# Transposes of the output rows in the places of u and v, and a later start for one row's sums and the other row's scores

## The chip, the cores and the metric

The kernel runs on one core of a Trainium2 chip. The time is the device time of one execution in microseconds (us). Before the change the median of three runs is 1711.06 us (1710.57 to 1711.61). The engines are TensorE (PE, its weight loads PEld), VectorE (DVE), ScalarE (ACT), GpSimd (POOL) and SyncE (SP), which issues most of the transfers.

## The reference

Sixteen rows of 512 positions by 512 features go through two layers, each added to its input.

```python
# layer 0: two dense layers; the last 128 outputs come from the row's own expert
h = gelu(einsum('bnd,hd->bnh', x, fc1_w) + fc1_b)             # hidden 2048
shared = einsum('bnh,sh->bns', h, fc2_w) + fc2_b               # 384 outputs
expert = einsum('bnh,bph->bnp', h, experts_w[idx]) + experts_b[idx]  # 128 outputs
x = x + concatenate([shared, expert], -1)
# layer 1: attention pooling with one score per position
scores = einsum('bsa,a->bs', tanh(einsum('bsd,da->bsa', x, W1) + b1), v)
mask = where(pt == 0, l <= j, where(pt == 1, l >= j, l != j))  # per row one of three
p = softmax(where(mask, scores[:, None, :], -1e30), -1)
x = x + einsum('bjl,bld->bjd', p, x) / mask.sum(-1)
```

All of it is float32. The masked softmax has only prefix, suffix and all-but-one forms, so the pooling is written as recurrences along the positions (scans on VectorE) and no product of 512 by 512 is made.

## The kernel before

**Groups.** Rows are worked in pairs, eight groups of an *elder* row (`b0`) and a *younger* row (`b0 + 1`). The products use a seven-product scheme for 2 by 2 blocks (1, 5, 6, 2, 7, 3, 4 in the order of work), so operands need sums and differences, made on VectorE or GpSimd. A group has a first stage (lines 1456 to 1506: seven outer by seven inner products, Gelu into `hT`) and a second one. In groups 1 to 6, called joint, the second stage has an upper part for both rows at once (`Joint.upper`, steps u0 to u13) and then for each row five products named 5, 7, 6, 3 and 4 (`Joint.row`). "Row 0" and "row 1" below are these row parts of the elder and the younger row. Groups 0 and 7 use `fc2` instead.

**One product of a row** (line 1004) is 32 matmuls into one bank: 16 with the shared weights (m = 0) and 16 with the row's expert weights (m = 1). In the middle of each half and between them a callback runs, named by the product and a letter: `5a` after a quarter, `5m` after half, `5c` after three quarters, and `5` after the outputs have been taken. What the callback `at_row` issues stands at that place in every engine's queue. The whole order is written out by hand: each engine works strictly in the order in which the program issues, and only semaphores are inserted.

**What the callbacks issue.** `joined.outer(r, k)` (line 982) makes row r's four moving operands, one VectorE instruction of 128x2048 each (line 987): k = 0 for product 5, 1 for product 7, 2 for product 6, 3 for product 4. `sum1` (line 519) and `sums` (lines 522 to 530) make the expert's weight sums; `sums("a11", h)` is needed by the m = 1 halves of 7 and 6, `sums("a12", h)` by that of 3. Both take a tile from the ring. `residual` (line 714) loads a piece of the input on ScalarE's queue and adds the bias there. The row's four output quarters are written at lines 1012, 1027, 1031 and 1034 into `x1T`, of which there are two buffers.

**The ring.** Weight tiles of 256 KB come through ten buffers in the order of one written plan (`Ring`, lines 176 to 198); a freed buffer lets SP issue the next load of the plan. SP's queue also holds the stores of the outputs and, once per group, the eight loads of the next group's `x` (`Moving`, line 290), whose place comes free with line 1012 of row 1.

**Pooling.** A row's `Pooling` begins with `project` (line 1059, eight matmuls and a tanh on ScalarE) and `score` (line 1069, two matmuls, two copies into `srow`, a transfer into `s2`). The rest is a generator. Its first part makes coefficients with many small VectorE instructions, stores them (`co`, lines 1290 and 1291) and reads them back broadcast to all partitions (`cb`, line 1295; a copy at 1298). Then, for four chunks of the features, come `weigh` (1326 on VectorE, 1329 on ScalarE), `recur` (1337, a scan, then 1363 and 1364 on ScalarE) and `finish` (1345 and 1355), each step fed by the one before. Last come two small instructions on GpSimd (1388, 1389) and, for rows below 13, four transposes on VectorE (`flip`, line 1405), each with four stores of 64 KB in packets of 128 bytes (line 1410).

The generator is advanced by `slot(budget, passed)`: each yielded number is a cost against the budget, a negative number a pause. The tables `SPARE`, `JOINT_0` and `JOINT_1` give the budgets per place, and only the oldest pooling advances. `drain(left)` issues at once all that is left: `drain(1)` just before row 0 ends the previous group's elder pooling, and `drain()` just after row 0's last product ends the previous group's younger one. The elder row of the current group is projected and scored within row 1, the younger one in the first block of the next group's first stage.

**Where the transposed chunks are put.** `flip` takes a tile of tag `yo` of which there are two buffers. The two `srow` tiles of a pooling have the same tag, and one of them is kept until the maximum search of that pooling (lines 1194 and 1196). The tags `u` and `v` are tiles of 128 x 1024, one buffer each, used by `weigh` and `recur`.

Of the kernel before, what the change touches and what calls it, by code (L numbers as in the profile page):

```python
# [9 lines left out]
F32 = mybir.dt.float32  # L10
# [7 lines left out]
def tile_cond_experts_then_prompt_pool(  # L18
# [17 lines left out]
    P = 128  # L36
    B, _, ND, S = xT.shape
# [21 lines left out]
    p1 = ctx.enter_context(tc.tile_pool(name="p1", bufs=1))  # L59
# [12 lines left out]
    LOWER = ("s1", "s3", "s2", "s4", "a22")  # L72
# [5 lines left out]
    def joint(i):  # L78
        return 0 < i < B // 2 - 1
# [95 lines left out]
    class Ring:  # L175
        def __init__(self):
            self.plan, self.tiles = [], {}
            for i in range(B // 2):
                b = 2 * i
                for o in OUTER:  # L180
                    self.plan += [("f1", i, o, p) for p in (INNER if i else INNER_0)]
                if joint(i):
                    ex = lambda r, o: [("ex", b + r, o, h) for h in range(2)]
                    lo = lambda r, names: [("lo", b + r, n, h) for n in names for h in range(2)]
                    u = [("u2", b, o, n) for o in ("a11", "a12") for n in UPPER]
                    self.plan += u[:10] + ex(0, "a11") + u[10:]
                    for r in range(2):
                        self.plan += (ex(1, "a11") if r else []) + lo(r, LOWER[:1]) + ex(r, "a12") + lo(r, LOWER[1:])
                    continue
                for r in range(2):  # L190
                    self.plan += [("up", b + r, "a11", h) for h in range(4)]
                    if not r:
                        self.plan += [("ex", b, "a11", h) for h in range(2)]
                    self.plan += [("up", b + r, "a12", h) for h in range(4)]
                    self.plan += [("ex", b + r, "a12", h) for h in range(2)]
                    self.plan += [("lo", b + r, n, h) for n in LOWER for h in range(2)]
                    if not r:
                        self.plan += [("ex", b + 1, "a11", h) for h in range(2)]
            self.at = 0
            self.taken, self.free = [], set()  # L200
# [346 lines left out]
    ex = const.tile([SG, 96], F32, name="ex")  # L547
# [166 lines left out]
    def residual(b, r, c):  # L714
        t = p1.tile([P, 2, HC], F32, tag="xr", name=f"xr_{b}_{r}{c}", bufs=2)
        nc.scalar.dma_start(t, xT[b][:, ts(r, 2), ts(c, HC)])

        def ready():
            for m in range(2):
                oc = 2 * r + m  # L720
                bias = fc2b_sb[:, oc : oc + 1] if oc < NS else be[:, b : b + 1]
                nc.scalar.activation(t[:, m, :], t[:, m, :], AF.Identity, bias=bias)  # L722
            return t

        return ready
# [320 lines left out]
    class Pooling:  # L1046
# [101 lines left out]
        def run_all(self):  # L1148
            yield from self.weights()
            yield from self.apply()  # L1150
            if self.b < B - 3:
                yield -2
                for dc in range(ND):
                    store = self.flip(dc)
                    yield 0.7
                    yield -1
                    store()
                    yield -1

        def weights(self):  # L1160
            V, b = nc.vector, self.b
# [239 lines left out]

        def flip(self, dc, yo=None):
            if yo is None:
                yo = p1.tile([P, S], F32, tag="yo", name=f"yo_{self.b}_{dc}", bufs=2)
            nc.vector.transpose(yo, self.x1T[:, dc, :])  # L1405
            to = out[self.b].rearrange("(c j) (k a i) -> k a j c i", j=32, a=4, i=32)

            def store():
                for a in range(4):
                    nc.sync.dma_start(to[dc, a], yo[ts(a, 32), :].rearrange("j (c i) -> j c i", i=32))  # L1410

            return store
# [15 lines left out]
    def drain(left=0):  # L1428
        while sum(not p.done for p in pools) > left:
            slot(1e9, 1e9)  # L1430
# [7 lines left out]
    }  # L1438

    JOINT_0 = {"5c": 1.0, "5": 2.0, "7c": 1.5, "7": 2.5, "6a": 1.5, "6m": 2.5, "3a": 1.5, "3m": 1.0, "3": 2.0}  # L1440
    JOINT_1 = {"5": 1.5, "7a": 1.5, "7c": 1.2, "7": 1.5, "6a": 1.5, "6": 0.4, "4a": 1.2}

    LAST_2 = {n + q: 1.7 for n in "57633" for q in ("a", "m", "c", "")}
    LAST_2.update({"6": 0.4, "3a": 0.8, "3m": 0.8})
    pool = xi_after = None
    for i in range(B // 2):
# [4 lines left out]
        experts = Expert(b0)  # L1451
# [4 lines left out]
        for n in range(7):  # L1456
# [8 lines left out]
            for k in range(14):  # L1465
# [28 lines left out]
                if n == 6 and joint(i):  # L1494
                    if k == LAG:
                        joined = Joint(b0, hT)
# [18 lines left out]
        if joint(i):  # L1515
            nxt, xr = {}, {}

            def at_upper(name):
                if name == "u0":
                    joined.sum("a11", 2)  # L1520
                elif name == "u1":
                    for h in range(2):
                        experts.sum1(h)
                elif name == "u2":
                    xr_next[:] = [t() for t in xr_next]
                elif name == "u4":
                    joined.outer(0, 0)
                elif name == "u7":
                    xr["22"], xr["12"] = residual(b0, 1, 1), residual(b0, 0, 1)
                elif name == "u8":  # L1530
                    joined.outer(0, 1)
                elif name in ("u9", "u10"):
                    experts.sums("a11", int(name[1:]) - 9)
                elif name in ("u11", "u12"):
                    n = ("22", "12")[int(name[1:]) - 11]
                    xr[n] = xr[n]()
                    slot(1.2, 1.7)

            def at_row(r, name):
                if name == "5m":  # L1540
                    joined.outer(r, 2)
                elif name == "7m":
                    joined.outer(r, 3)
                if r == 0:
                    if name == "5a":
                        for h in range(2):
                            experts.sums("a12", h)
                    elif name == "7":
                        nxt["ex"] = Expert(b0 + 1)
                        for h in range(2):  # L1550
                            nxt["ex"].load(h)
                    elif name == "6c":
                        joined.outer(1, 0)
                    elif name == "3m":
                        for h in range(2):
                            nxt["ex"].sum1(h)
                    elif name == "3c":
                        joined.outer(1, 1)
                    elif name == "4m":
                        for h in range(2):  # L1560
                            nxt["ex"].sums("a11", h)
                    elif name == "4a":
                        for n in ("22", "12"):
                            nxt[n] = nxt[n]()
                    slot(JOINT_0.get(name, 0.0), 1.7)
                    return
                if name == "5a":
                    pool.project()
                    nxt["x"] = Moving(i + 1)
                elif name == "5m":  # L1570
                    pool.score()
                    pools.append(pool)
                    for h in range(2):
                        experts.sums("a12", h)
                elif name == "6m":
                    nxt["xi"] = nxt["x"].inner_sums(0, nc.vector)
                    nxt["x"].outer_sum(1, nc.vector)
                elif name == "3m":
                    nxt["xi_2"] = nxt["x"].inner_sums(1, nc.vector)
                slot(JOINT_1.get(name, 0.0), 1.7)  # L1580

            def after(r):
                if r == 0:
                    nxt["22"], nxt["12"] = residual(b0 + 1, 1, 1), residual(b0 + 1, 0, 1)
                else:
                    b = b0 + 2
                    xr_next[:] = [residual(b, 0, 0), residual(b + 1, 0, 0) if joint(i + 1) else residual(b, 1, 1)]

            ba = joined.upper(xr_next, at_upper)
            drain(1)  # L1590
            for r in range(2):
                x1T = joined.row(
                    r, ba[r], experts, nxt if r else xr, lambda name: at_row(r, name), lambda: after(r)
                )
                if r == 0:
                    experts = nxt["ex"]
                    drain()
                before_last, pool = pool, Pooling(b0 + r, x1T)
            x_next, xi_next, xi_after = nxt["x"], nxt["xi"], nxt["xi_2"]
            continue  # L1600
        for row in range(2):
            b = b0 + row
            more = row == 1 and b + 1 < B
            nxt = {}
# [68 lines left out]
            if row == 0:  # L1673
                experts = nxt["ex"]
# [3 lines left out]
            before_last, pool = pool, Pooling(b, x1T)  # L1678
# [46 lines left out]
```

## Time and profile before

| what | value |
|---|---|
| median of three runs | 1711.06 us |
| the profiled execution's own time, and its span | 1713.13 us, 1711.3 us |
| TensorE busy, its weight loads | 1580.4 us, 1313.3 us |
| VectorE busy | 1242.7 us |
| ScalarE busy, GpSimd busy | 626.5 us, 453.5 us |
| mean granted TensorE clock | 0.964 |
| VectorE's idle time ahead of line 1405, put down to the stores | 105.0 us in 33 waits |
| ScalarE's idle time ahead of line 1012, put down to line 1405 | 82.3 us in 5 waits |

A line of the groups or of the timeline reads: line, engine, operation, output<-inputs, shape, count, busy time, and in brackets the idle time of the engine ahead of it with what ended it. The waits list sums such idle time by who waited for whom. A wait for several things is put down to the one that came last. Names stand without their numbers: `w_lo_s` is any tile of the ring for the products 5, 7, 6 and 3 of a row, `pa` the projection's bank, `psc` the score's.

### The profile page before, as it was taken

Reading aid. Unit: us, or ns where it says so; the run is one execution under the profiler, and the core shown is the slowest. Engines: PE = TensorE matmul, PEld = TensorE weight load, DVE = VectorE, ACT = ScalarE, POOL = GpSimd, SP = SyncE. Lnnn points to the kernel's source line nnn. Section 1 sums busy time; section 2 is a strip of 40 time slices with the busy share of each in tenths; the row PEclk is TensorE's granted clock in tenths of the full one; section 3 lists DMA queues with packets and bytes.
Section 4 is the critical chain, followed back from the end, with each engine's and each line's share of the span. In section 5 each row is a group of like instructions: output and inputs, shape, how many; then the busy total and the mean of one; then the engine's idle time right before and its main releaser. Section 6 shows DMA issues by size and latency. Waiting matters only on the chain. (4 is left out here: it accounts for less than half of the span.)

```text
span 1711.3 us, 22082 instructions
## 1 busy us (share of the span) xinstructions
PE 1580.4 (92%) x6890; PEld 1313.3 (77%) x6890; DVE 1242.7 (73%) x2200; ACT 626.5 (37%) x1304; POOL 453.5 (26%) x440
## 2 busy tenths in 40 slices
PE   8999999999999699997999979999699987998996
PEld 6788888877888488875888758887588875886784
DVE  7885668766887659866598665986659877586686
ACT  2441246322561325513265022641226412363323
POOL 5631045000631016300263001620117201260020
PEclk9999999999999899998999989999899998999997
DMA  7768646546556375563655636556365664555442
GB/s 261 239 203 273 219 129 175 173 127 223 152 155 179 91 235 153 160 175 93 226 150 168 184 95 212 148 170 193 85 205 148 178 179 126 181 149 155 141 118 49
DMA packets 344768, 285.60 MB, mean 167 GB/s; under 512 B 145356, under 2 KB 262156, under 8 KB 344652
## 3 DMA queue, kind: packets, MB, share of 16 engines
q1 hardware_dynamic: 313388, 241.09, 48.9%
q10 hardware_dynamic: 24864, 21.04, 3.8%
q0 software_dynamic: 6400, 22.07, 3.6%
q8 instruction: 55, 0.90, 0.2%
q14 instruction: 61, 0.50, 0.1%
HBM read 252.50 MB, written 31.55 MB: 166 GB/s over the span
## 5 line engine op out<-in xcount | busy, mean ns | idle before, releaser
L633 ACT ACTIVATE hT<-hT,fc1b_sb 128x256 f32<-128x256 f32 x416 | 181.2, 501 | 59.8 <-DVE hT L687 34.5
L674 POOL TENSOR_TENSOR q<-p,hT 128x512 f32<-128x512 f32 x80 | 105.5, 1320 | 347.0 <-ACT p L667 346.6
L616 PE MATMUL bx<-xi,w_f_s_s 128*128 128x256 f32 x512 | 128.0, 382 | 3.3 <-DVE by L671 1.7
L1405 DVE STREAM_TRANSPOSE yo<-x1T 128x512 f32<-128x512 f32 x60 | 41.2, 701 | 107.4 <-DMA out_y<-yo 105.0
L616 PEld LDWEIGHTS bx<-xi,w_f_s_s 128*128 128x128 f32 x512 | 96.0, 190 | 21.5 <-issue 3.6
L671 DVE TENSOR_TENSOR by<-bx,p 128x512 f32<-128x512 f32 x112 | 77.4, 691 | 39.3 <-PE bx L616 38.7
L616 PE MATMUL bx<-xi,w_f_a_s 128*128 128x256 f32 x384 | 97.3, 386 | 3.2 <-POOL xi L337 2.6
L1337 DVE TENSOR_TENSOR_SCAN f<-cb,u 128x512 f32<-128x512 f32 x60 | 81.8, 1363 | 22.3 <-ACT u L1329 21.6
L1063 PE MATMUL pa<-x1T,w_sb 128*128 128x512 f32 x120 | 65.7, 687 | 33.9 <-DVE x1T L1034 32.1
L646 DVE TENSOR_TENSOR hT<-bx,hT 128x512 f32<-128x512 f32 x112 | 75.1, 682 | 23.1 <-PE bx L616 23.0
L1146 POOL TENSOR_TENSOR xm<-x1T,is 128x4 f32<-128x4 f32 x15 | 5.3, 352 | 310.2 <-DVE wt L1210 263.7
L1004 PE MATMUL bd<-hT,e 128*128 128x256 f32 x384 | 86.8, 379 | 0.0
L667 ACT COPY p<-bd 128x512 f32<-128x512 f32 x112 | 65.3, 583 | 58.5 <-PE bd L616 57.2
L616 PEld LDWEIGHTS bx<-xi,w_f_a_s 128*128 128x128 f32 x384 | 71.7, 191 | 19.1 <-POOL xi L337 4.8
L1345 DVE TENSOR_TENSOR f<-v,cb 128x512 f32 x60 | 54.1, 902 | 41.6 <-ACT v L1364 41.6
L1004 PEld LDWEIGHTS bd<-hT,e 128*128 128x128 f32 x384 | 73.0, 190 | 9.9
L646 DVE TENSOR_TENSOR hT<-by,hT 128x512 f32<-128x512 f32 x112 | 75.0, 681 | 3.7 <-PE by L616 1.3
L722 ACT ACTIVATE xr<-xr,fc2b_sb 128x256 f32<-128x256 f32 x96 | 44.3, 502 | 85.9 <-DMA xr<-in_xT 30.1
L1363 ACT ACTIVATE v<-f,U,cb 128x512 f32<-128x512 f32 x60 | 48.8, 813 | 69.6 <-DVE U L1338 68.8
L1063 PEld LDWEIGHTS pa<-x1T,w_sb 128*128 128x128 f32 x120 | 25.0, 215 | 61.7 <-DVE x1T L1034 37.0
L687 DVE TENSOR_TENSOR hT<-bx,q 128x512 f32<-128x512 f32 x80 | 54.6, 682 | 18.8 <-PE bx L616 17.2
L662 ACT COPY ba<-bx 128x512 f32<-128x512 f32 x32 | 18.3, 571 | 133.3 <-PE bx L616 110.5
(351 smaller groups left out, 3938.9 us busy)
## 6 DMA issues: line engine op xcount, KB each, us to landing
w_lo_s<-w2s_s SPq DMA_DIRECT2D x128, 256.0 KB
w_f_s_s<-w1s_s_s SPq DMA_DIRECT2D x112, 256.0 KB
w_f_a_s<-w1s_a_s SPq DMA_DIRECT2D x84, 256.0 KB
w_f_s_a<-w1s_s_a SPq DMA_DIRECT2D x84, 256.0 KB
w_f_a_a<-in_fc1T SPq DMA_DIRECT2D x69, 256.0 KB
w_ex_a<-in_fc2T SPq DMA_DIRECT2D x64, 256.0 KB
xr<-in_xT ACTq DMA_DIRECT2D x64, 256.0 KB
out_y<-yo SPq DMA_DIRECT2D x240, 64.0 KB
```

What stands on the lines that cost most here:

```text
L616: nc.tensor.matmul(to.rearrange("p (b s) -> p b s", b=2) if len(mv.shape) == 3 else to, w[:, ts(2 * mh + m, P)], mv, start=(not add and m ...
L633: nc.scalar.activation(to[:, m], src[:, m], AF.Gelu, bias=fc1b_sb[:, hc + m : hc + m + 1])
L646: eng.tensor_tensor(to, src, self.place(prev, r, c, mh)[1], ALU.add)
L667: nc.scalar.copy(u["p5"], bd)
L671: add(u["y"], u["x"], u["p5"], ALU.add)
L674: nc.gpsimd.tensor_tensor(self.both(u["q"]), self.both(u["p5"]), self.place(self.to[0][1], 1, 1, mh)[1], ALU.add)
L687: add(to, self.both(u["x"]), self.both(u["q"]), ALU.add)
L1004: nc.tensor.matmul(bank[:, m, :], ex.of(n)[:, k, :] if m else as_chunks(lo[k // 4])[:, k % 4, :], mv[:, k, :], start=(not add and m == 0 a ...
L1063: nc.tensor.matmul(pa, w1_sb[:, dc, :], self.x1T[:, dc, :], start=(dc == 0), stop=(dc == ND - 1))
L1337: V.tensor_tensor_scan(f[dc], c0, turned(u[dc]), 0.0, ALU.mult, ALU.add)
L1345: V.tensor_tensor(f[dc], turned(v[dc]), beta, ALU.mult)
L1363: nc.scalar.activation(v[dc][:, :S], f[dc], AF.Identity, bias=U[:, dc : dc + 1], scale=fac)
```

## The change

The transposes get a new place: chunks 0 and 1 share one tile of tag `u`, chunks 2 and 3 one of tag `v`, so `yo` is left to the score rows (and to the start and the last row). The pause after each store is gone. For a group's younger row, `outer(1, 1)`, which row 0's product 3 used to issue, is issued in row 1's product 5 (at 5a), and the expert's a11 sums move from row 0's product 4 to row 1's 5m; `outer(1, 2)` moves from 5m to 5c and the a12 sums from 5m to 7c. The plan of the ring puts the a11 tiles of the younger row behind its s1 tiles, and the a12 tiles behind s3. The elder row's projection moves from 5a to 5m and its score from 5m to 7a, and the budgets of row 1 follow.

```diff
@@ Ring.__init__
-                    for r in range(2):
-                        self.plan += (ex(1, "a11") if r else []) + lo(r, LOWER[:1]) + ex(r, "a12") + lo(r, LOWER[1:])
+                    self.plan += lo(0, LOWER[:1]) + ex(0, "a12") + lo(0, LOWER[1:])
+                    self.plan += lo(1, LOWER[:1]) + ex(1, "a11") + lo(1, LOWER[1:2]) + ex(1, "a12") + lo(1, LOWER[2:])
@@ Pooling.run_all
                     store()
-                    yield -1
@@ Pooling.flip
-                yo = p1.tile([P, S], F32, tag="yo", name=f"yo_{self.b}_{dc}", bufs=2)
+                if dc % 2 == 0:
+                    self.yo = p1.tile([P, 2, S], F32, tag=("u", "v")[dc // 2], name=f"yo_{self.b}_{dc}")
+                yo = self.yo[:, dc % 2, :]
@@ budgets
-    JOINT_1 = {"5": 1.5, "7a": 1.5, "7c": 1.2, "7": 1.5, "6a": 1.5, "6": 0.4, "4a": 1.2}
+    JOINT_1 = {"5": 1.5, "7": 1.5, "6a": 1.5, "6": 0.4, "3a": 1.2, "4a": 1.2}
@@ at_row
-                if name == "5m":
-                    joined.outer(r, 2)
-                elif name == "7m":
+                if name == "7m":
                     joined.outer(r, 3)
                 if r == 0:
-                    if name == "5a":
+                    if name == "5m":
+                        joined.outer(r, 2)
+                    elif name == "5a":
...
-                    elif name == "3c":
-                        joined.outer(1, 1)
-                    elif name == "4m":
-                        for h in range(2):
-                            nxt["ex"].sums("a11", h)
...
                 if name == "5a":
-                    pool.project()
+                    joined.outer(r, 1)
                     nxt["x"] = Moving(i + 1)
                 elif name == "5m":
+                    pool.project()
+                    for h in range(2):
+                        experts.sums("a11", h)
+                elif name == "5c":
+                    joined.outer(r, 2)
+                elif name == "7a":
                     pool.score()
                     pools.append(pool)
+                elif name == "7c":
                     for h in range(2):
                         experts.sums("a12", h)
```

## The prediction

> **What bounds the kernel now.** First the page's busy shares and the clock row.
>
> ```profile
> span 1711.3 us, 22082 instructions
> PE 1580.4 (92%) x6890; PEld 1313.3 (77%) x6890; DVE 1242.7 (73%) x2200; ACT 626.5 (37%) x1304; POOL 453.5 (26%) x440
> PEclk9999999999999899998999989999899998999997
> ```
>
> TensorE carries the kernel, and its granted clock dips at regular places. The last chain (section 4 of the page) covers only the tail, so I went to the waits of TensorE alone:
>
> ```profile
> PE psc L1072 <- ACT aT L1067: 36.8, 6, 7.5
> PE pa L1063 <- DVE x1T L1034: 32.1, 6, 6.5
> PE ba L1004 <- DVE hT L987: 15.8, 6, 3.6
> PE bc L766 <- DMA w_lo_s<-w2s_s: 8.1, 1, 8.1
> ```
>
> Columns: total us, times, longest. Three waits come once in each of the six joint groups, 84.7 us in all; the fourth is in group 7. Where they come from is seen in the timeline of one group (group 2: start, us, engine, idle before it and its releaser):
>
> ```profile
> 524.35 3.62 PE L1004 MATMUL bc<-t,w_lo_s 128*128 128x256 f32 x16
> 536.15 0.71 DVE L1405 STREAM_TRANSPOSE yo<-x1T 128x512 f32<-128x512 f32 x1 [3.64 <-DMA out_y<-yo]
> 540.30 3.72 PE L1004 MATMUL ba<-hT,w_lo_s 128*128 128x256 f32 x16 [1.97 <-DVE hT L987]
> 553.99 0.37 SPq L1295 DMA_DIRECT2D cb<-co_d  x1
> 561.15 1.05 ACT L1298 COPY cb<-cb 128x1024 f32<-128x1024 f32 x1 [12.13 <-DMA cb<-co_d]
> 562.83 0.67 DVE L1326 TENSOR_TENSOR u<-x1T,cb 128x512 f32<-128x512 f32 x1
> 565.94 0.61 ACT L1329 ACTIVATE u<-u 128x512 f32<-128x512 f32 x1
> 570.22 0.68 DVE L1034 TENSOR_TENSOR x1T<-bd,u 128x512 f32<-128x512 f32 x1
> 570.96 3.70 PE L1063 MATMUL pa<-x1T,w_sb 128*128 128x512 f32 x4 [6.23 <-DVE x1T L1034]
> 583.63 1.87 PE L1072 MATMUL psc<-aT,v_sb 128*1 128x512 f32 x2 [7.25 <-ACT aT L1067]
> 585.42 5.02 PE L1004 MATMUL bc<-t,es 128*128 128x256 f32 x16
> 590.28 3.62 PE L1004 MATMUL bd<-hT,w_lo_s 128*128 128x256 f32 x16
> 593.10 0.71 DVE L1405 STREAM_TRANSPOSE yo<-x1T 128x512 f32<-128x512 f32 x1 [3.29 <-DMA out_y<-yo]
> 618.20 1.03 PE L616 MATMUL bx<-xT,w_f_a_a 128*128 128x256 f32 x4
> ```
>
> Row 0's products start at 524.35. Meanwhile VectorE is held in the transposes of the previous group's elder row, each waiting for the store before it (4.22, 3.31 and 3.64 us), and is free only at 536.9. From there it runs without a gap to 562.8, so all of row 0's work is late: TensorE waits 1.97 us for a difference, the younger pooling's coefficients go out at 553.99, and L1034 comes at 570.22. The projection waits for it. The score then waits for a tanh that ScalarE has behind the drained pooling. The transposes after 584.84 wait for stores again.
>
> A product is two halves of 3.45 us; ten of them, a projection (3.60) and a score (1.02) are 73.6 us. Group 2 took 618.20 - 524.35 = 93.85. The same difference, from the same lines, is 80.2, 95.65, 95.9, 96.7 and 93.7 us for groups 1, 3, 4, 5, 6.
>
> **The change part by part.**
>
> *Transposes into u and v.* Each group's elder drain loses three waits on stores. Its four transposes (0.65 us apart) now end behind the last upper addition (L976, released by TensorE's end at 524.35): about 526.5 instead of 536.9. The younger drain loses 2.97 + 3.29. The new owners wait for nothing: the last readers of u and v are the steps just before on VectorE and ScalarE, and the next weighing comes tens of us after the stores.
>
> *The dropped pause* shortens the elder pooling in the budget tables, but followed slot by slot it only moves its first transpose from the last block of stage one to u11; the younger's steps in row 0 keep their slots in groups 2 to 6. In group 1 they come some eight slots earlier. Worth nothing by itself in 2 to 6; its cover is the 89 us of stage one.
>
> *Row 0, group 2, with VectorE 10.4 us earlier.* Same durations: expert sums 1.25, L987 2.27, steps 1.7, p5x 0.6, steps 2.0, L987 2.27, steps 1.2 end at 537.7; then L1019 waits for TensorE (product 7 ends 538.2), and the remaining 4 us of coefficients end at 543. TensorE no longer waits and ends product 6 at 545.1; SP then issues two loads and the broadcast at 546.3 (553.99 before). It took 7.2 us to its copy, so cb is ready at 554.6. Residuals: L1024 frees their place at 546 instead of 555.3, so they land 9.2 us earlier and ScalarE weighs at 556.7 (565.94). Sums and difference (2.4 + 2.27) are gone from ahead of it. So L1034 moves by 9.2 to 561.0.
>
> *Row 1.* It starts at 558.9. The projection stands after 16 matmuls (562.4), its second half at 564.2: L1034 is done, that wait is gone. The score stands in product 7, behind a tanh ready by 574: gone. **The stall goes to product 7.** Its operand, outer(1, 1), is now issued after the whole drain. L1034 to the drain's first transpose took 584.84 - 570.22 = 14.6 us; four transposes 2.65, L987 2.3: ready at 561.0 + 19.5 = 580.5. TensorE is there at 558.9 + 6.9 + 3.6 = 569.4, so it waits 11.1 us. Queued behind the moved difference on VectorE are the expert sums (2.5), outer(1, 2) (2.3), p5x, the a12 sums and outer(1, 3): all end within 9 us, and the second half of product 7, product 6 and product 3 need theirs 3.4, 8.9 and 16 us on.
>
> *Clock.* After the 7.25 us wait, the score took 1.87 for 1.02 and the next half product 5.02 for 3.62: 2.25 us lost. After 3.44 us in group 3, 5.41 for 3.62; after 3.64 in group 4, nothing. The Trainium skill (TensorE: Matmul & The Clock Gate, Part 1: The HAM clock gate) has half clock after an idle window of about 3.4 us and until a busy one: 1.7 us per long wait however long it is, by its free-running window more or less. Row and rule are near; I take 2.3 by the row (the rule gives 0.6 less per group). One long wait in place of two pays it once.
>
> So row stage = 45.0 + 11.1 + 2.3 + four products 27.6 + score 1.0 = **87.0 us**. For groups 2 to 6: 475.8 before - 435.0 = 40.8 saved. In group 1 the pooling is one chunk further, its drain ends about 369, outer(1, 1) at 371, and TensorE needs it at 373.9: all 6.4 us over 73.6 vanish.
>
> *Loads.* In the new plan s4 and a22 of the younger row stand on SP behind 16 stores and 8 loads of x. Stores: 16 took 9.49 us in group 1; from 576.3 to 586, x to 590, s4 by 591.5. TensorE needs s4's halves at 597 and 598.7. In group 1's trace a22, issued behind x at 394.26, had its second half awaited at 403.8, 9.5 us on: that would be 600, a wait of 1.4. The skill (DMA: Bandwidth & Descriptors, Queues, rings and completion order) has SP own one row of rings and the engines take turns between rows: only the 2.6 MB ahead on SP's own row count in full, at the 320 to 400 GB/s of group 1's windows 7 to 8 us after x's first issue and some start-up: 595 to 596, no wait. The expert gathers that shared group 1's engines come later here. I take half, 0.7 us for six groups: 4 lost. Bounds 0 and 4 us a group.
>
> x itself lands by 596 and is needed in VectorE's 6m step; hidden. ScalarE's copies of scores (11 us behind stores before) are free; nobody waits.
>
> *Elder steps later* (new budgets in row 1): some 10 small VectorE steps and the issues of co move to the first block of stage one; the broadcast comes 3 slots later and is needed 8 slots after that. Nothing; without that cover the 7 us of a broadcast.
>
> *Group 7.* TensorE's 8.1 us wait is for two loads behind 16 stores, which took 15.69 us gated by transposes; ungated about 10, so 5 of 8.1 come back. 5 us.
>
> Sum: 40.8 + 6.4 - 4 + 5 = 48. The profiled execution's own time is 1713.1 (1.8 around its span): 1665.1. It lies 2.1 above the median of the runs, so on their scale **1663 us**.
>
> **Rivals.**
> 1. *The younger chain comes forward by half only*, because broadcast and residuals, now in the traffic of denser stores, take longer than 7.2 and 8.4 us. For: those two, not VectorE, released the chain. Against: engines moved 60 to 70% then. Each us is one us in five groups: 4.6 x 5 = 23, so 1686.
> 2. *s4 comes late* by its upper bound, 4 us a group: 20 more, 1683. For: the order on SP; against: the bytes.
> 3. *Slower: the transposes still wait*, since two share one place; if the order is kept for a whole tile, the second waits for the first one's store. Elder drain: some 7 us kept, so the chain comes 7 later; younger drain: 6.3 kept in front of outer(1, 1). Row stage 87.0 + 13.3 = 100.3, 5.1 over the mean of 95.2: +26 in five groups; group 1 gains 3, group 7 some 2, loads cost 4: 1736. It decides from 8.2 us of kept waits a group. Against: at 562.85 half of the projection ran on two quarters of x1T with L1034 unwritten, so order is kept for parts of a tile.
> 4. *Better*: product 7 waits only 8 us, loads cost nothing: 1644.
> 5. *Nothing moves*: the stall at product 7 equals the two removed.
>
> **How the numbers follow.** Likeliest 54% (own range 1648 to 1678: 3 us a group either way), rival 1 15%, rival 2 11%, rival 3 or a stall of like size 13%, rival 4 4%, rival 5 3%. Leaving out rival 3, the far end of rival 1 and the best of rival 4 gives 1645 to 1698. A difference within 0.2%, 3.4 us, can't be told from none. Faster: 54 + 15 + 11 + 4 = 84%; same 3%; slower 13%.
>
> **What would show it.** L1405 without waits on out_y; no wait at L1063 and L1072; L1004's bd of row 1 waiting about 11 us for L987 in groups 2 to 6, none in group 1; L1034 some 37 us after row 0's start (46 now); row stages near 87. Wrong if L987 is awaited 18 us or more, if bc of row 1 waits for a DMA of w_lo, or if L1405 still waits.

## The result and the profile after

The changed kernel takes **1728.17 us** (median of four runs, 1727.85 to 1730.19) against 1710.82 beside it: a ratio of 1.0109 with a 95% interval of 1.0094 to 1.0124. It is slower by some 17 us where 1663 was forecast, so the prediction was wrong in sign.

The head of the page after, the same three rows as before:

```profile
span 1726.2 us, 22078 instructions
PE 1572.7 (91%) x6890; PEld 1313.5 (76%) x6890; DVE 1236.0 (72%) x2200; ACT 622.0 (36%) x1304; POOL 430.5 (25%) x440
PEclk9999999999999899998999989999899998999997
```

Nothing shows in the shares; the clock row has as many dips as before. TensorE's waits (total us, times, longest) show what changed places:

```profile
PE bd L1004 <- issue: 63.3, 5, 13.8
PE bc L1004 <- DMA w_lo_s<-w2s_s: 21.2, 5, 5.9
PE pa L1063 <- DVE x1T L1034: 15.4, 5, 3.5
PE bc L766 <- DVE ml L1184: 7.2, 1, 7.2
...
PE psc L1072 <- ACT aT L1067: 2.1, 1, 2.1
```

The tanh wait (36.8 before) is down to 2.1, and the wait for differences in row 0 is gone. The new first line is product 7 of row 1: no releaser is named, but its matmul starts 0.11 us after the moved difference ends (586.50 + 2.25 against 588.86, below). The second line is product 3 of row 1 waiting for an s4 tile (s4 are its shared weights, a22 those of product 4); that wait did not exist before. The third was to vanish and has halved.

Group 2 in the timeline of TensorE and SP (start, us, engine, line, operation; idle before and releaser in brackets). Row 0 starts at 527.33, and a time with a plus sign below is counted from the start of row 0:

```profile
527.33 3.62 PE L1004 MATMUL bc<-t,w_lo_s 128*128 128x256 f32 x16
...
552.39 0.94 SPq L238 DMA_DIRECT2D w_ex_a<-in_fc2T  x2
553.42 0.45 SPq L1289 DMA_DIRECT2D co_d<-co  x1
...
556.67 0.32 SPq L1294 DMA_DIRECT2D cb<-co_d  x1
...
569.49 0.68 DVE L1034 TENSOR_TENSOR x1T<-bd,u 128x512 f32<-128x512 f32 x1
570.22 1.98 PE L1063 MATMUL pa<-x1T,w_sb 128*128 128x512 f32 x4 [3.02 <-DVE x1T L1034]
...
584.83 13.89 SPq L1412 DMA_DIRECT2D out_y<-yo  x16
...
586.50 2.25 DVE L987 TENSOR_TENSOR hT<-hT 128x2048 f32<-128x2048 f32 x1
...
588.86 3.75 PE L1004 MATMUL bd<-hT,w_lo_s 128*128 128x256 f32 x8 [13.20 <-issue]
...
598.82 4.05 SPq L262 DMA_DIRECT2D xT<-in_xT  x8
...
602.97 0.90 SPq L236 DMA_DIRECT2D w_lo_s<-w2s_s  x2
...
610.48 6.59 PE L1004 MATMUL bc<-hT,w_lo_s 128*128 128x256 f32 x16 [4.65 <-DMA w_lo_s<-w2s_s]
...
627.27 1.03 PE L616 MATMUL bx<-xT,w_f_a_a 128*128 128x256 f32 x4
```

Two things are late against the forecast. The coefficients' store (`co`) goes out 26.1 us after the row's start and the broadcast (`cb`) at 29.3, although TensorE no longer waits in row 0; so L1034 is at +42.2, not +36.7. And the 16 stores start late and take 13.89 us, x follows, and the s4 tile is issued at +75.6 and used at +83.2. In group 2 the waits are 3.02 + 13.20 + 4.65, and the slow clock behind them costs 1.96 (3.75 and 1.99 for two quarters of 1.89) and 2.97 (6.59 for 3.62): with 73.6 that is 99.4 of the stage's 99.94. The clock rule that the prediction weighed (1.7 us per long wait, an estimate from the window on the page that it names: half of 3.4 us) is near the first and low for the second. The trace's records have the clock at half from 578.81 to 592.47 and from 609.53 to 616.36: 3.6 us of matmuls ran at half after the first wait and 5.9 us after the second.

What SP waited for in that window, 527 to 560 us, and over the whole execution of the kernel after:

```profile
SPq L238 <- DMA xr<-in_xT: 10.5, 1, 10.5
...
SPq L1412 <- DMA xr<-in_xT: 59.3, 13, 7.7
SPq L238 <- DMA xr<-in_xT: 50.4, 5, 10.5
```

and over the whole of the kernel before:

```profile
SPq L1410 <- DMA xr<-in_xT: 9.8, 5, 7.7
SPq L238 <- DMA xr<-in_xT: 3.4, 1, 3.4
```

This is the surprise. A load of an expert tile on SP waits 10.5 us for a *residual*, a load of another tile on another queue, whose data it has nothing to do with; there are five such waits in the execution. What the two share is in the records of the transfers: each carries the number of a semaphore, and the transfers of SP and ScalarE take eight of these in turn (108, 111 to 116, 118). A stretch of group 2 after, sorted by the turn, not by time:

```
issued   engine    line   transfer            semaphore
538.30   SP        1412   out_y<-yo           118
549.02   ScalarE    716   xr<-in_xT           108
538.66   SP        1412   out_y<-yo           111
549.57   ScalarE    716   xr<-in_xT           112
539.19   SP        1412   out_y<-yo           113
539.80   SP         238   w_lo_a<-in_fc2T     114
540.34   SP         238   w_lo_a<-in_fc2T     115
540.90   SP         236   w_lo_s<-w2s_s       116
541.45   SP         236   w_lo_s<-w2s_s       118
552.39   SP         238   w_ex_a<-in_fc2T     108
552.87   SP         238   w_ex_a<-in_fc2T     111
553.42   SP        1289   co_d<-co            112
```

The residual with 108 can't go out before product 6 frees its place (549.02), yet in the turn it stands among stores of 538. The next transfer with 108, SP's expert tile, waits for it, and `co`, `cb` and the ring's loads stand behind it in SP's order. The records have both ends: the residual's sixteenth and last update of number 108 comes at 552.33, and SP's wait for 108 ends at 552.34. Before the change the same residuals had 115 and 116, behind `cb` (114), and held nothing that mattered. The Trainium skill (DMA: Bandwidth & Descriptors, Anatomy of one DMA, a section on GpSimd's path that says this of the DMA engines as such) has a transfer's wait done on the issuing sequencer and not by the DMA engines; the trace agrees for SP, since all that is queued on SP behind L238 stays for 10.5 us.

### The profile page after: what moved, and what is told of

Read it like the earlier page. It is cut to its first block, busy times and chain, and to the rows that moved or that the text cites. A ratio compares the mean times of both kernels' runs of the same rounds, so it can differ in the third digit from the quotient of the medians.

```text
span 1726.2 us, 22078 instructions
## 1 busy us (share of the span) xinstructions
PE 1572.7 (91%) x6890; PEld 1313.5 (76%) x6890; DVE 1236.0 (72%) x2200; ACT 622.0 (36%) x1304; POOL 430.5 (25%) x440
## 5 line engine op out<-in xcount | busy, mean ns | idle before, releaser
L1004 PE MATMUL bd<-hT,w_lo_s 128*128 128x256 f32 x192 | 54.4, 439 | 63.3 <-issue 63.3
L1004 PEld LDWEIGHTS bd<-hT,w_lo_s 128*128 128x128 f32 x192 | 41.3, 221 | 78.4 <-issue 72.1
L646 DVE TENSOR_TENSOR hT<-bx,hT 128x512 f32<-128x512 f32 x112 | 75.3, 684 | 31.8 <-PE bx L616 31.8
L1325 DVE TENSOR_TENSOR u<-x1T,cb 128x512 f32<-128x512 f32 x60 | 54.2, 903 | 40.6 <-DMA w_lo_s<-w2s_s 16.1
L1004 PE MATMUL bc<-hT,w_lo_s 128*128 128x256 f32 x192 | 53.5, 441 | 26.3 <-DMA w_lo_s<-w2s_s 21.2
L1063 PE MATMUL pa<-x1T,w_sb 128*128 128x512 f32 x120 | 58.0, 620 | 15.9 <-DVE x1T L1034 15.4
L662 ACT COPY ba<-bx 128x512 f32<-128x512 f32 x32 | 18.2, 570 | 149.3 <-PE bx L616 138.8
L1004 PEld LDWEIGHTS bc<-hT,w_lo_s 128*128 128x128 f32 x192 | 42.8, 226 | 36.0 <-DVE ex L1224 11.8
```

Source lines behind the costliest of these rows:

```text
L646: eng.tensor_tensor(to, src, self.place(prev, r, c, mh)[1], ALU.add)
L1004: nc.tensor.matmul(bank[:, m, :], ex.of(n)[:, k, :] if m else as_chunks(lo[k // 4])[:, k % 4, :], mv[:, k, :], start=(not add and m == 0 a ...
L1063: nc.tensor.matmul(pa, w1_sb[:, dc, :], self.x1T[:, dc, :], start=(dc == 0), stop=(dc == ND - 1))
L1325: V.tensor_tensor(u[dc][:, :S], x1T[:, dc, :], c1, ALU.mult)
```

## The experiments

Two theories stood first. **Theory 1**: the gain went to the held issues of `co` and `cb`, and with them to later stores, x and s4. **Theory 2**: the moves (operand and sums behind the drain) are the price, whatever queue anything is on. All eleven kernels compute the whole reference. For each, the time, the ratio to the kernel before on the same chip, and from the profile, as means over groups 2 to 6: the issue of `co` and the start of L1034 after row 0's start, the time from the younger row's first store to the end of its sixteenth, and the two row parts from row 0's start to the next stage; the last column is that of group 1 alone.

| kernel | us | ratio (95%) | co | L1034 | 16 stores | rows 2 to 6 | group 1 |
|---|---|---|---|---|---|---|---|
| before | 1710.82 | | 28.4 | 47.1 | 8.9 | 95.2 | 80.2 |
| after | 1728.17 | 1.0109 (1.0094 to 1.0124) | 25.8 | 42.2 | 14.1 | 98.8 | 80.7 |
| e1_flips_only | 1687.29 | 0.9886 (0.9867 to 0.9906) | 25.6 | 42.2 | 11.5 | 90.4 | 77.8 |
| e2_moves_only | 1754.26 | 1.0273 (1.0256 to 1.0290) | 28.6 | 46.3 | 8.7 | 103.4 | 85.8 |
| e3_outer_back | 1737.97 | 1.0178 (1.0161 to 1.0195) | 25.7 | 42.4 | 13.0 | 100.6 | 84.1 |
| e4_residuals_pool | 1694.69 | 0.9928 (0.9903 to 0.9953) | 18.2 | 35.0 | 14.3 | 92.0 | 79.7 |
| e11_co_pool | 1694.94 | 0.9920 (0.9892 to 0.9947) | 18.5 | 36.3 | 14.1 | 92.7 | 81.3 |
| e6_x_later | 1689.24 | 0.9886 (0.9859 to 0.9913) | 25.7 | 42.0 | 14.0 | 92.3 | 73.6 |
| e5_pool_x_later | 1654.09 | 0.9685 (0.9657 to 0.9713) | 18.2 | 34.9 | 14.4 | 85.5 | 73.6 |
| e8_before_pool | 1709.83 | 1.0005 (0.9987 to 1.0023) | 27.8 | 45.7 | 8.9 | 94.5 | 80.9 |
| e7_flips_scores_pool | 1647.18 | 0.9638 (0.9611 to 0.9664) | 18.2 | 36.6 | 9.3 | 84.4 | 75.3 |
| e9_scores_pool_x | 1620.05 | 0.9475 (0.9457 to 0.9492) | 18.2 | 36.1 | 9.3 | 77.7 | 74.4 |
| e10_outer_pool_x | 1616.07 | 0.9461 (0.9443 to 0.9478) | 18.2 | 35.2 | 9.4 | 77.9 | 73.6 |

**The residuals on another queue (e4_residuals_pool).** Against the changed kernel:

```diff
-    def residual(b, r, c):
+    def residual(b, r, c, queue=nc.scalar):
...
-        nc.scalar.dma_start(t, xT[b][:, ts(r, 2), ts(c, HC)])
+        queue.dma_start(t, xT[b][:, ts(r, 2), ts(c, HC)])
...
-            xr["21"] = residual(b, 1, 0)
+            xr["21"] = residual(b, 1, 0, nc.gpsimd)
...
-                    nxt["22"], nxt["12"] = residual(b0 + 1, 1, 1), residual(b0 + 1, 0, 1)
+                    nxt["22"], nxt["12"] = (residual(b0 + 1, k, 1, nc.gpsimd) for k in (1, 0))
```

> The changed kernel with the residual loads of the row parts issued on GpSimd's queue instead of ScalarE's; all else as changed. Theory 1: co goes out at once when the coefficients are ready (about +19 us after the row's start instead of +26) and cb at +20 to +22 instead of +29, L1034 at +37 instead of +42, the stores of the younger drain are not held by a residual (16 in about 10 us instead of 13.9), s4 is awaited less than 1 us; row stages near 87 to 92, total 1665 to 1695. Theory 2: the residuals' queue does not matter, co and cb go out as late as before or their gain is lost elsewhere: total 1720 to 1735.

33 us faster than the changed kernel; Theory 2 falls. In the records GpSimd's transfers carry other semaphores (99 to 106; these residuals 100, 101, 102 and 105). In group 2, where row 0 starts at 526.28, the two that were held before go out at 548.45 and 549.19, +22.2 and +22.9 (+21.7 and +22.2 in the changed kernel), and `co` is no longer behind them:

```profile
538.10 0.94 SPq L238 DMA_DIRECT2D w_ex_a<-in_fc2T  x2
544.50 0.33 SPq L1289 DMA_DIRECT2D co_d<-co  x1
...
547.62 0.32 SPq L1294 DMA_DIRECT2D cb<-co_d  x1
...
576.36 14.03 SPq L1412 DMA_DIRECT2D out_y<-yo  x16
590.49 4.05 SPq L262 DMA_DIRECT2D xT<-in_xT  x8
594.64 1.24 SPq L236 DMA_DIRECT2D w_lo_s<-w2s_s  x2
```

L1034 comes at +35.0 and the projection's wait is gone. But Theory 1's other half missed: the stores still take 14 us, and s4 is awaited for 26.8 us in six groups where less than 1 us each was expected. So there is a second, separate price: s4 itself. TensorE's first two waits in this kernel:

```profile
PE bd L1004 <- issue: 46.7, 5, 10.3
PE bc L1004 <- DMA w_lo_s<-w2s_s: 26.8, 6, 7.3
```

**The coefficients on another queue (e11_co_pool),** residuals left where they were ("Theory A" in this expectation is that `co` is late through the order on SP alone):

```diff
-            self.queue = nc.gpsimd if b == B - 2 else nc.sync
+            self.queue = nc.gpsimd if b % 2 or b == B - 2 else nc.sync
```

> The changed kernel with the coefficients' stores and the broadcast (co, sc, cb) of the younger rows on GpSimd's queue; the residuals stay on ScalarE's, x and s4 as changed. Theory A (co is late only because it stands on SP behind a load that waits for a residual of its completion semaphore): SP's load of the expert tile is held as before, co goes out at +18 to +20 us after the row's start instead of +26, L1034 at +36 to +38, product 7's wait near 10 us, s4 some 4 to 5 us earlier but still late, as in e4_residuals_pool: total 1693 to 1705. If the traffic at that time were the reason, and not the order on SP, co or its landing stays late: 1720 to 1730.

Two views of this kernel in group 2, SP's waits from 525 to 558 us and GpSimd's timeline (row 0 starts at 525.35):

```profile
SPq L238 <- DMA xr<-in_xT: 10.3, 1, 10.3
```

```profile
543.80 0.62 POOL L1289 DMA_DIRECT2D co_d<-co  x1 [2.00 <-DVE q L1280]
...
547.59 0.58 POOL L1294 DMA_DIRECT2D cb<-co_d  x1 [2.60 <-DMA co_d<-sc]
```

SP is held just as long, and `co`, no longer queued behind that load, goes out when VectorE has made it. The time is that of e4. The place of `co` on SP behind a held load is the cause, and not the traffic of the residuals.

**The residuals moved in the kernel before (e8_before_pool),** the same edit as e4's:

> The kernel before with the residuals of the row parts on GpSimd's queue and nothing else. There co waits for no residual, so both theories expect no change: 1704 to 1714. A gain of 20 us or more would say that the gain of e4_residuals_pool over the changed kernel has nothing to do with the change.

No change, so e4's gain belongs to the changed kernel.

**x behind s4 (e6_x_later, e5_pool_x_later).** Once it was seen that s4 stays late, two new theories: **Theory A**, the held issues and s4's place on SP behind 16 stores and x are two prices; **Theory B**, s4's wait is only where the stall shows. e6 has this edit to the changed kernel alone, e5 has it with e4's:

```diff
                 if name == "5a":
                     joined.outer(r, 1)
+                elif name == "5":
                     nxt["x"] = Moving(i + 1)
```

> The changed kernel with the loads of the next x after row 1's product 5, residuals on ScalarE's queue as changed. Theory A: co and cb stay held (L1034 at +42 after the row's start), product 7's wait stays at 13 us, s4 comes about 4 us earlier and its wait of 21.2 us falls to about 3: total 1695 to 1710. Theory B: 1720 to 1730.

> As e4_residuals_pool (residuals of the row parts on GpSimd's queue), and the eight loads of the next x are issued after row 1's product 5 instead of in it, so the two s4 tiles stand on SP ahead of x, behind the 16 stores alone. Theory A (two things cost what was forecast as gain: the held issues of co and cb, and s4 on SP behind the stores and x): s4 goes out about 4 us earlier, its wait of 26.8 us in six groups falls below 8 and the slow clock behind it goes; row stages of groups 2 to 6 near 87, total 1660 to 1675. Theory B (only the held issues cost, s4's wait is just where a stall shows up): the wait appears elsewhere in row 1 and the total stays at 1690 to 1697.

Each edit alone gains 33 (e4) or 39 us (e6) over the changed kernel, both together 74: the two prices add. e6 and e5 each beat Theory A's range by 6 us; Theory B falls. In e5 no wait for s4 is left among TensorE's waits in the row parts:

```profile
PE bd L1004 <- issue: 46.6, 5, 9.9
PE bc L766 <- DMA w_lo_s<-w2s_s: 7.6, 1, 7.6
...
PE psc L1072 <- ACT aT L1067: 2.1, 1, 2.1
```

The stall at product 7 is 9.3 us per group (forecast 11.1), the row stages are 85.5 (87.0) and group 1 is 73.65 (73.6). e5 behaves as the prediction said that the changed kernel would.

**The operand back in row 0 (e3_outer_back, e10_outer_pool_x).** The same edit, to the changed kernel and to e5:

```diff
+                    elif name == "3c":
+                        joined.outer(1, 1)
...
-                    joined.outer(r, 1)
```

> The changed kernel with the operand of row 1's product 7 made in row 0's product 3 again, before the drain. The wait of 13.2 us at product 7 goes; product 6's operand is now the first behind the drain and is needed 7 us later, so 5 to 6 us of wait stay there. Theory 1: L1034 stays at +42 to +44, the stores and s4 stay late: about 7 us a group in five groups, 1690 to 1700. Theory 2: the moves were the price, so about 11 us a group or more, 1670 to 1680.

> As e5_pool_x_later, with product 7's operand of row 1 made in row 0's product 3 again, before the drain: e3_outer_back's edit in a kernel in which neither co nor s4 is held. In e3 it gained nothing, since s4 came at +84.6 us whatever stood before it. Theory A: here the wait of 9.3 us at product 7 goes, product 6's operand is needed 7 to 8 us later, so 1 to 2 us of it stay and the clock loss goes; five row stages of 85.5 fall to 76 to 79, total 1610 to 1630. If the moved operand earns its price in the chain, L1034 comes 2 us later and the projection waits: 1640 to 1655.

e3 missed both theories: it is *slower* than the changed kernel. The wait at product 7 is gone, and TensorE stands at product 3 instead (group 2, row 0 from 528.64):

```profile
580.24 1.89 PE L1004 MATMUL bd<-hT,w_lo_s 128*128 128x256 f32 x8
585.15 1.86 PE L1072 MATMUL psc<-aT,v_sb 128*1 128x512 f32 x2 [3.02 <-ACT aT L1067]
...
613.51 6.14 PE L1004 MATMUL bc<-hT,w_lo_s 128*128 128x256 f32 x16 [12.14 <-DMA w_lo_s<-w2s_s]
```

s4 is used at +84.9 here and at +83.2 in the changed kernel, whatever stood before it: with s4 behind the stores and x, the drain's stores set the end of the row stage, and the stall of 13 us that the changed kernel has at product 7 costs nothing there. Why e3 is even slower is open in part: on the mean of groups 2 to 6 its s4 goes out no later (+75.2 against +76.2), but product 3 starts 1.3 us later, and what follows it takes 0.6 us more. With both prices taken away (e10) the same edit gains 38 us over e5. Its waits:

```profile
PE psc L1072 <- ACT aT L1067: 11.2, 6, 2.8
PE bd L1004 <- DVE e L527: 8.8, 5, 2.3
PE bc L766 <- DMA w_lo_s<-w2s_s: 7.6, 1, 7.6
```

The clock row of its page has no dip left in the row stages:

```profile
PEclk9999999999999999999999999999999999999998
```

e10 also explains the long stores. SP's waits in group 2 of e5 and then of e10, both from 566 to 592 us:

```profile
SPq L1412 <- DMA s<-srow: 4.3, 1, 4.3
```

```profile
SPq L1412 <- DMA s<-srow: 0.5, 1, 0.5
```

This is the same turn again: a store takes the number after ScalarE's transfer of the scores, which follows the score matmul, which stands behind product 7's stall. Without the stall 16 stores take 9.4 us. In the changed kernel a residual (L716, issued at 593.99 with number 112) is waited for in the same place, 4.2 us in group 2.

**One half of the change at a time (e1_flips_only, e2_moves_only).** e1 is the kernel before with the new `flip` and without the pause; e2 is the changed kernel with these two taken back:

```diff
                     store()
-                    yield -1
...
-                yo = p1.tile([P, S], F32, tag="yo", name=f"yo_{self.b}_{dc}", bufs=2)
+                if dc % 2 == 0:
+                    self.yo = p1.tile([P, 2, S], F32, tag=("u", "v")[dc // 2], name=f"yo_{self.b}_{dc}")
+                yo = self.yo[:, dc % 2, :]
```

> The kernel before with the transposes in u and v and without the pause; sums, scores, differences and plan stay as they were. Theory 1 (the change loses because SP's issues of co and cb, and later of x and s4, are held behind ScalarE's residual loads, with which they take completion semaphores in turn): what this kernel does depends on where the residuals fall in that turn; the transposes lose their waits, L1034 of row 0 comes at +36 to +43 us after the row's start instead of +46, and as nothing is queued before product 7's operand there is no wait of 13 us in row 1: row stages of groups 2 to 6 near 82 to 90, total 1640 to 1680. Theory 2 (the moved sums, differences and scores are the price): the flips alone gain what was forecast for them, L1034 at +37, row stages near 80, total 1630 to 1650.

> The changed kernel with the transposes back in yo and the pause back: only the moves of sums, differences and scores, the plan and the budgets. Both theories have the transposes wait for stores again, about 10 us in each drain, and product 7's operand of row 1 behind the younger drain: row stages near 105, total about 1760. Theory 1: most of the loss over the kernel before is at product 7 (20 us of wait there). Theory 2: the same; a total at or below 1728 would say that the flips, not the moves, are what costs.

A line of TensorE's waits in e1, then one in e2:

```profile
PE psc L1072 <- ACT aT L1067: 35.8, 6, 7.3
```

```profile
PE bd L1004 <- issue: 101.7, 6, 19.3
```

The flips alone gain 1.1%, the moves alone lose 2.7%, with a stall at product 7 of 17 us in the mean of six groups (20 expected). On top of the flips the moves cost 2.3% (1.0109 over 0.9886). So much of Theory 2 is true: the operand behind the drain has a price of its own, which the forecast had in its sum, and e10 wins it back. e1 came out 7 us above its range: both theories had overlooked that the score still waits for a tanh behind the drained pooling (35.8 us in six groups, as before). Theory 2's 1630 to 1650 failed in e1 for another reason too: `co` at +25.6, as in the changed kernel. In its group 2 the residuals have numbers 108 and 112 as in the changed kernel, and a load on SP waits 9.5 us for one. So the held issues come with the flips and the dropped pause; in e2, with the moves alone, the numbers of the group's residuals fall behind `cb` as before (115 and 116 against 114). Why the turn is dealt differently with the flips is not seen in any of these traces.

**The flips and the later scores, without the other moves (e7_flips_scores_pool, e9_scores_pool_x).** e7 is e1 with e4's edit and

```diff
                 if name == "5a":
-                    pool.project()
                     nxt["x"] = Moving(i + 1)
                 elif name == "5m":
-                    pool.score()
-                    pools.append(pool)
+                    pool.project()
...
+                elif name == "7a":
+                    pool.score()
+                    pools.append(pool)
```

with the new `JOINT_1`; e9 has x behind product 5 as well.

> The kernel before with the transposes in u and v, without the pause, the elder row's projection at 5m and score at 7a with the new budgets of row 1, and the residuals of the row parts on GpSimd's queue; product 7's operand, the sums of both kinds and the plan stay where they were. Theory A: nothing stands ahead of product 7, s4's tiles are loaded long before the stores, L1034 comes at +37 to +41 and delays only the projection by 0 to 3 us; row stages near 75 to 80, total 1610 to 1640. Theory B gives the same here; if the moved sums were needed to bring the chain forward, L1034 stays at +42 or later and the total at 1650 or above.

> As e7_flips_scores_pool, with the loads of the next x after row 1's product 5, so a22's tiles stand ahead of x. If a22 is late in e7 because it stands behind x (2.0 us of wait in group 2 and a half product of 5.38 for 3.62 behind it), that wait of 17.4 us and its slow clock go: five row stages of 84.4 fall to 79 to 81, total 1622 to 1635. If it is late through the stores alone, 1640 to 1648.

e7 missed by 7 us: a22, not s4, stands behind x in the old plan:

```profile
PE bd L1004 <- DMA w_lo_a<-in_fc2T: 17.4, 5, 5.3
```

e9 takes that away and comes out 2 us below its range. e9 and e10 differ by 4 us: where the a11 and a12 sums and the other operands are made hardly matters once row 1's product 7 has its operand before the drain and the flips, the later score and the two queue edits are there. The fastest kernel, e10, takes 0.9461 of the time before.

## Why the prediction was wrong

**Right.** The transposes no longer wait for stores: rival 3 is out, and that its 1736 lies near the measured time is chance. VectorE's coefficients are ready when forecast: in e4, where nothing holds it, `co` goes out at +18.2 in group 2 (544.50 - 526.28); the forecast's own end of the coefficients, 543 on a row that starts at 524.35, is +18.7. The wait for the difference of product 6 vanishes, and that for tanh but for 2.1 us. The stall goes to product 7 and is 12.7 us (forecast 11.1), and its place behind the whole drain is as described. The later sums cost nothing: e9 and e10 are equal within 4 us.

**The step that failed first: "SP then issues two loads and the broadcast at 546.3".** It took SP as free because the trace of before showed it waiting there for VectorE alone, mostly for the coefficients, and for no transfer. The first line of SP's waits before, 524 to 556 us:

```profile
SPq L1290 <- DVE q L1281: 9.6, 1, 9.6
```

On the changed kernel's clock that would be 549.3 (22.0 us after the row's start); the broadcast went out at 556.67. The first of those two loads waited 10.5 us for a residual, through a semaphore that they take in turn. L1034 came at +42.2, not +36.7: of the 9.2 us that the chain was to move, 3.7 did. It is rival 1 in its effect (23 us named there, 33 measured by e4 against the changed kernel), but not by its mechanism: the broadcast's own time did not grow, its issue was held.

**The step that failed second: the loads, "from 576.3 to 586, x to 590, s4 by 591.5", bounds 0 and 4 us a group.** This is rival 2, and it was mis-sized; the prediction's own sign for it, bc of row 1 waiting for a DMA of w_lo, came true. All terms but that of x were too small. The stores start 5.5 us later since the chain is; they take 14.1 us (mean of five groups) and not 9.49, since one of them waits for a transfer of ScalarE in the same turn (4.2 us in group 2); x takes the 4 us that were forecast. So s4 is issued at +75.6 in group 2 instead of +67. From issue to use it takes 7.5 us, where the forecast had 3.5 to 4.5 (595 to 596 after 591.5) by the bandwidth and 9.5 by group 1's trace. e6, which only takes x from in front of it, gains 39 us. The 4 us of s4's wait in the list of waits (21.2 in five groups) are the smallest part of it, since most of s4's lateness lay under product 7's stall: e3 brings it to light as 12 us. The prediction weighed bytes and bandwidth; of the lateness of s4 at its use in group 2, 8.5 us of some 12 lie before its issue, in the order on SP, and only the rest between issue and use.

**Group 1: "all 6.4 us over 73.6 vanish".** (80.2 less 73.6 is 6.6.) They did only where x is behind s4 (73.65 in e5, e6 and e10). In the changed kernel there is no stall at product 7, as forecast, but product 3 waits 5.10 us and its half runs at 5.38 for 3.62:

```profile
397.60 5.38 PE L1004 MATMUL bc<-hT,w_lo_s 128*128 128x256 f32 x16 [5.10 <-DVE ex L1224]
```

The profile names a small step of the pooling as what came last; the s4 loads went out at +57.3 and +58.0, 7 to 8 us before the use at +65.1, and with x behind them, in e6, the wait is gone.

**Group 7: "ungated about 10, so 5 of 8.1 come back".** 0.9 came back: 7.2 us of wait remain, and 7.6 in e5 and e10. The 16 stores take 14.16 us where 15.69 was; they are freed of the transposes, and one waits for a residual instead (5.9 us).

**Sum.** Forecast 48 us of gain, measured 17 of loss: 65 us between. e5 takes away the two failed steps and lands at 1654 us, 9 below the forecast, so these two hold the whole difference; the forecast's other terms were right to some 10 us in their sum. The range failed because it gave SP's queue two bounded terms and no case in which both are late at once.

## What to carry to other kernels

Before a transfer is taken to go out "when its data is ready", look at what stands in front of it on the queue that issues it, and what each of these may wait for, buffers and completion semaphores included; an issue that is queued behind a load with a late place waits with it. When a plan moves a load behind stores, count from the start of the stores in the new schedule, and ask of a stall in front of that load whether it costs anything at all: undoing the stall alone, as in e3, can gain nothing.

A change that is slower may hold a large gain: two small edits in the queues turned +1.1% into -3.2%, and one operand's place then made it -5.4%.

## What was not expected of the hardware

Transfers of SP and of ScalarE are coupled in this program: eight semaphores are taken in turn over both queues, and a transfer isn't issued until the one before it with the same number has landed (10.5 us for a load that shared nothing else with it; 59.3 us in 13 waits for the stores of one execution). Which number a transfer has stands in the program, and the flips with the dropped pause, no edit of any load, changed it. Transfers from GpSimd's queue are outside this turn (numbers 99 to 106): moving four loads of a group there is worth 33 us in the changed kernel and nothing in the kernel before.
